# Layer 1's two lists of steps put into another order

## The chip, the cores and the metric

The kernel runs on one core of a Trainium2 chip. The metric is the time of one execution in microseconds (us) on the device. The kernel before took 2359.34 us, the median of three runs (2358.97 to 2359.86).

A core has engines that run side by side, each through its own instructions in order: PE (TensorE, matrix products and transposes), DVE (VectorE), ACT (ScalarE), POOL (GpSimd) and SP (SyncE, which here only issues DMAs). ACT and POOL issue DMAs too. An instruction that has to wait for another engine or for a transfer holds up all that stands behind it on its own engine. PSUM is the memory that PE writes its results to; it has eight banks of 128 x 512 numbers here.

## The reference, cut to what matters

The input x is 8 batches of 512 channels and 1024 tokens (32 x 32), all float32. Layer 0 is a GroupNorm, attention with 8 heads, a projection and a residual. The change leaves it alone. Layer 1 takes the output of layer 0:

```python
xf = x.reshape(B, C, N)
q, kk, v = wq @ xf, wk @ xf, wv @ xf                    # per batch, 512 x 512 weights
importance = nan_to_num(sum(xf * xf, axis=1))
_, topk_idx = top_k(importance, 256)
q_sel, k_sel, v_sel = q[topk], kk[topk], v[topk]        # 256 tokens x 512
q_sel, k_sel = layer_norm(q_sel), layer_norm(k_sel)
attn = softmax(clip(nan_to_num(q_sel @ k_sel.T * C ** -0.5), -80, 80))
out = v.at[topk].set(attn @ v_sel)                      # other tokens keep their v
return x + (wo @ out).reshape(B, C, H, W)
```

So each batch of layer 1 ranks its 1024 tokens by their squared length, runs attention among the best 256, and writes the result back into the values of all tokens.

## The kernel before

Layer 0 ends, and layer 1 begins, at about 1910 us. Layer 1 works batch by batch. One batch is cut into small steps; each is a function (lines 277 to 675) named by a word and a number, such as `row3` or `exp0`. The steps of a batch, in the order in which data passes through them:

- load (L243, SP) brings x of a batch, 2 MB in four chunks; the trace calls the chunks x, x_q, x_k. Two batches can be held; the load of the next one waits until the last reader of the old one is done.
- row 0 to 7 (L277, PE) transposes 128 tokens, four transposes into one PSUM bank; square (L282, ACT) writes squares into a tile xT and sums them; keep (L289, ACT) overwrites xT with the tokens; put (L293, a DMA issued by ACT, 256 KB) writes xT to device memory (sx). There are four xT tiles, so a square waits until the put four back has landed.
- finite (L296, DVE), spread (L304, PE, four transposes), imp (L312, ACT) and count (L317, DVE, eight steps) rank the tokens. place, pick (DVE), holder (PE) and who (DVE) turn ranks into the list of the best 256 tokens.
- xs (L402, POOL) builds sums of blocks of x; va to vf (L412, PE) compute the values of all tokens in seven products a quarter (Strassen-like), with the weights Wv and Wo already multiplied; va is eight matmuls, each other one four. ka, kb, kc, ke (L426, ACT) and kf, kg, kd (L430, DVE) take the results to V. vput (L437, a DMA issued by ACT, 256 KB) writes V to device memory (sv).
- getx and getv (L476, POOL) gather the chosen rows of x and V, two indirect DMAs each.
- selt (L500, PE) transposes the gathered x, selk (L508, ACT) copies it, qk 0 to 3 (L516, PE, 4 matmuls of 512 columns) computes queries and keys; stats (DVE), root (L534, ACT), norm (L539, DVE), normt (L555, PE) and scale (L565, ACT) are the layer norm.
- score (L577, PE), clip (L587, DVE), exp (L600, ACT), probt (L611, PE), probk (L619, ACT), att (L626, PE) and attk (L634, ACT) are the attention; attput (L641, SP) writes the result to device memory (sa); fetch 0 to 7 (L647, POOL, indirect DMAs) copies the result rows over the chosen rows of V.
- back 0 to 7 (L660, PE) transposes V; add (L670, DVE) adds the residual and issues the output DMA and the load of a later residual on SP.

Every PE step that writes PSUM takes a bank from a ring of eight (class Ring): the bank freed first is taken first, and it is freed by a named step (`keep`, `imp`, `selk`, `norm`, `scale`, `clip`, `probk`, `attk`, `add`, the last value copy, `who`). So a step of PE can also wait for a copy that belongs to quite another step.

The order of all this is written out by hand. `BATCH` (L65) is one iteration of the steady state, 180 words; `END` (L79) is the last stretch, 462 words, in which batches 4 to 7 run out. A word's number is the step's index; each "-" means one batch behind and each "+" one batch ahead of the iteration's batch. `layer1` (L700) expands them:

```python
for t in range(-1, B - 2):
    if 1 <= t:
        steps.append(("load", t + 1, 0))
    steps += [(name, t + ahead, i) for name, ahead, i in order
              if 0 <= t + ahead and (t + ahead or name not in EARLY)]
steps.append(("load", B - 1, 0))
steps += [(name, B - 1 + ahead, i) for name, ahead, i in in_order(END)]
```

The steps are then issued in this order under a manual schedule: each engine and each DMA queue executes its own steps in the order of the list, and waits only for data, tiles and banks. So what matters of a list is the order of the words that belong to one engine, and how much work of that engine lies between a step and what it waits for. In this text, (5,0) behind a step's name means batch 5, index 0.

Of the kernel before, what the change touches and what calls it, by code (L numbers as in the profile page):

```python
# [62 lines left out]


BATCH = """  # L65
back6--- row3 square1 xs1 back4--- keep2 square3 back7--- va1 inv-- put2 va0 keep3 put4 row0
keep1 add6--- ka1 add7--- ka0 put1 put3 att0-- xs0 vb1 vb0 kb0 vc0 row6 square0 kb1 add4---
square6 holder- vd0 who- add3--- kc0 keep6 row7 keep0 row5 square5 kg0 vd1 att1-- keep5 square7
getx- keep7 ve0 finite kf1 kc1 attk1-- kf0 va2 attk0-- xs2 attput-- fetch7-- kd0 fetch4--
spread0 imp0 vc1 fetch3-- ka2 spread1 va3 selt0- imp1 selk0- count1 fetch6-- count7 selt1-  # L70
selk1- fetch2-- vb2 kg1 vf1 fetch5-- vput1- count4 kf2 qk1- ke1 count0 ve1 qk0- qk2- xs3 ka3
put0 stats1- vb3 kd1 root1- back5-- norm1- stats0- kb2 put7 vput2- vput4- fetch1-- count3 vput5-
add5-- stats2- root0- qk3- norm0- vd2 vput7- vput0- stats3- root2- kc2 fetch0-- back1-- kb3
root3- vf0 normt0- vput6- ke0 norm2- vd3 back2-- back0-- normt1- vput3- put5 add1-- scale0-
scale1- vc2 vf2 norm3- normt2- count6 ke2 getv- vc3 normt3- add2-- kc3 kg2 add0-- scale2- kg3
scale3- score0- count2 score1- put6 row4+ square4+ ve3 clip- row1+ row2+ keep4+ ve2 exp0- kd3
vf3 kd2 kf3 probt- count5 place back3-- pick1 square2+ pick0 ke3 probk-
"""
END = """  # L79
square1- inv--- row7- keep2- back6---- put4- row6- put2- keep1- square7- xs3- row3- row0-  # L80
att1--- put1- keep7- put7- square3- holder-- add3---- row5- attk1--- va3- keep3- square5- row0
keep5- square0- who-- square6- put5- back7---- back4---- vput2-- add7---- finite- add6----
att0--- keep6- spread0- spread1- getx-- add4---- ka3- imp0- row7 keep0- row1 selt0-- imp1- row4
selk0-- square7 selt1-- kf3- put3- put0- selk1-- keep7 count4- count3- vput7-- square4 square1
put7 keep4 xs2- qk0-- count0- attk0--- stats0-- qk1-- count6- va2- stats1-- keep1 attput---
put6- fetch5--- count5- ka2- root1-- kf2- square0 norm1-- keep0 vput4-- qk2-- vb3- vb2- put1
fetch1--- stats2-- put0 row2 kb2- row6 count2- put4 root2-- square2 vd2- square6 row3 kb3- qk3--
fetch7--- square3 keep2 fetch2--- norm2-- fetch6--- count1- kc2- vf2- root0-- vc2- norm0-- row5
vput6-- ke2- square5 kg2- keep3 normt0-- vd3- keep5 kc3- stats3-- root3-- vput1-- vc3- count7-
# [15 lines left out]
fetch6-- attput- score0 fetch2- kb3 add6-- vd3 fetch1- fetch0- va1 score1 fetch4- clip vsel0  # L105
back3-- back5-- ka1 vselk0 fetch6- kc3 kg3 exp0 ve2 fetch5- xs0 back1-- vf2 fetch7- add3-- probt
add1-- fetch3- va0 kd2 ke2 back2-- probk ka0 inv att0 att1 attk0 ve3 attk1 back7-- vb0 xs1 kb0
vb1 add5-- add2-- attput kb1 kf1 vc0 vd0 fetch2 back4- vd1 add7-- kc0 kc1 kf0 vf0 kg0 vc1 add4-
fetch6 kd3 ve0 back6- fetch3 kg1 ve1 kd0 ke0 back3- back1- add6- fetch4 fetch0 kd1 fetch1 vf1
# [1529 lines left out]
```

## Time and profile before

| | us |
|---|---|
| median of three runs | 2359.34 |
| the profiled execution | 2355.33 |
| its span, first to last instruction | 2353.0 |
| around the span | 2.33 |
| layer 1 in the trace | about 1910 to 2353 |
| one iteration of BATCH | 56.8 |
| PE busy in the span | 2317.2 (98%) |
| DVE, ACT, POOL busy | 1875.6, 1479.1, 1432.8 |
| granted TensorE clock, mean | 0.999 |

In the rows of a timeline the first number is the start in us, the second the length in us, then the engine, the line of the kernel, the operation with output and inputs by the program's names, the shape and the number of instructions put together in the row. A bracket at the end is idle time of the engine just before, with what ended it. Matmuls are pipelined, so a row of four that is 1.03 us long is followed by the next 0.87 us after its start. In a table of stages the columns are the stretch, its length, the busy time of each engine with the number of instructions, the granted clock (1.00 is full speed), the busy share of the DMA engines and what they moved in GB/s. In the chain of waits a DMA's length is the time from its issue to its landing.

### The profile page before, as it was taken

The page shows a single profiled execution, that of the slowest core. Times are in us where ns is not written, and L with a number is a line of the kernel's source. Part 1 is how long each engine was busy: PE and PEld are TensorE (multiplying, and loading weights), DVE is VectorE, ACT ScalarE, POOL GpSimd, SP SyncE. Part 2 cuts the span into 40 slices and gives each one's busy share as a digit, 9 for nine tenths or more (in the row PEclk, how much of TensorE's full clock was granted, in tenths as well). Part 3 has the DMA queues.
Part 4 walks back from the last instruction along what each step waited for, and adds up shares of the span by engine and source line. Part 5 has one row for each costly group of instructions (what it writes and reads, how often), then busy time and mean ns, then how long its engine had stood idle before and what let it go on. Part 6 is the DMA issues. An engine that isn't in the chain of part 4 may idle for free.

```text
span 2353.0 us, 36692 instructions
## 1 busy us (share of the span) xinstructions
PE 2317.2 (98%) x13164; PEld 1053.6 (45%) x13164; DVE 1875.6 (80%) x3020; ACT 1479.1 (63%) x2024; POOL 1432.8 (61%) x890
## 2 busy tenths in 40 slices
PE   7999999999999999999999999999999999999998
PEld 3333443344344334433443344334433357777766
DVE  4889988988898888888988898888787456777774
ACT  3678766776777577757776777677666534444632
POOL 2668655866676677657765776676556724444334
PEclk9999999999999999999999999999999999999999
DMA  5112222322231222222322222222323443666655
GB/s 197 48 44 67 75 76 70 102 69 73 79 96 53 82 82 89 59 79 79 91 69 77 89 82 60 84 68 55 102 82 117 139 170 118 224 217 226 225 171 173
DMA packets 201236, 244.41 MB, mean 104 GB/s; under 512 B 41930, under 2 KB 111306, under 8 KB 201056
## 3 DMA queue, kind: packets, MB, share of 16 engines
q1 hardware_dynamic: 175392, 198.51, 26.5%
q10 hardware_dynamic: 18144, 31.48, 3.7%
q0 software_dynamic: 7520, 12.09, 1.9%
q8 instruction: 104, 1.70, 0.3%
q14 instruction: 76, 0.62, 0.1%
HBM read 181.42 MB, written 73.14 MB: 108 GB/s over the span
## 4 chain that ended last, share of the span: by engine, by line
PE 89%; DVE 4%; DMA 2%; ACT 2%; issue 2%; POOL 1%; SPq 0%; ACTq 0%; DVEq 0%; POOLq 0%
PE sc L1278 19%; PE av L1358 17%; PE g L1034 15%; PE g L899 10%; PE g L1076 7%; PE b_px L412 4%; PE b_pp L520 4%; DVE high L1292 2%; PE b_py L412 1%; PE den L1374 1%; PE b_sc L582 1%; PE first L899 1%; PE b_pa L629 1%; DVE e L1339 1%; PE last L899 1%
## 5 line engine op out<-in xcount | busy, mean ns | idle before, releaser
L1347 POOL TENSOR_TENSOR es<-es,e 128x1024 f32<-128x1024 f32 x384 | 911.1, 2373 | 167.7 <-ACT e L1342 149.8
L1339 DVE TENSOR_TENSOR e<-e,ns 128x1024 f32<-128x1024 f32 x512 | 611.3, 1205 | 7.3 <-ACT ns L1335 7.3
L1286 ACT COPY e<-sc 128x1024 f32<-128x1024 f32 x512 | 501.7, 1016 | 170.2 <-DVE high L1292 101.7
L1342 ACT ACTIVATE e<-e 128x1024 f32<-128x1024 f32 x512 | 533.3, 1063 | 91.4 <-DVE e L1339 83.9
L1292 DVE TENSOR_TENSOR high<-sc,high 128x1024 f32<-128x1024 f32 x384 | 469.4, 1222 | 121.3 <-PE sc L1278 95.9
L1278 PE MATMUL sc<-q,k 64*128 64x512 f32 x2048 | 512.3, 617 | 4.1 <-DVE high L1292 2.5
L1358 PE MATMUL av<-e,v 128*64 128x512 f32 x2048 | 489.8, 598 | 0.6 <-ACT e L1342 0.5
L1347 POOL TENSOR_TENSOR es<-e,e 128x1024 f32<-128x1024 f32 x64 | 152.5, 2382 | 435.8 <-ACT e L1342 435.8
L1278 PEld LDWEIGHTS sc<-q,k 64*128 64x128 f32 x2048 | 174.5, 186 | 269.9 <-issue 146.9
L1358 PEld LDWEIGHTS av<-e,v 128*64 128x64 f32 x2048 | 135.8, 137 | 292.5 <-issue 235.2
L1034 PE MATMUL g<-wqkv,mix_qk 128*64 128x512 f32 x960 | 231.0, 602 | 1.3 <-POOL wqkv L944 1.3
L899 PE MATMUL g<-o,wp 128*64 128x512 f32 x912 | 206.8, 596 | 0.0
L1034 PE MATMUL g<-x,mix_qk 128*64 128x512 f32 x720 | 169.8, 593 | 0.2 <-ACT v L1093 0.2
L1034 PEld LDWEIGHTS g<-wqkv,mix_qk 128*64 128x64 f32 x960 | 60.9, 136 | 155.2 <-issue 115.7
L899 PEld LDWEIGHTS g<-o,wp 128*64 128x64 f32 x912 | 63.0, 137 | 135.4 <-issue 132.9
L520 PE MATMUL b_pp<-w,selT 128*128 128x512 f32 x256 | 114.0, 593 | 0.0
L1292 DVE TENSOR_TENSOR high<-sc,e 128x1024 f32<-128x1024 f32 x64 | 77.6, 1213 | 38.0 <-ACT e L1286 37.6
L1034 PEld LDWEIGHTS g<-x,mix_qk 128*64 128x64 f32 x720 | 51.6, 137 | 103.3 <-issue 89.7
L648 POOL DMA_INDIRECT V<-sa,at x64 | 64.6, 1009 | 54.1 <-issue 15.2
L426 ACT COPY V<-b_px 128x256 f32<-128x256 f32 x112 | 39.7, 374 | 88.4 <-PE b_px L412 81.2
L1410 POOL TENSOR_TENSOR o<-o,ri 128x512 f32<-128x512 f32 x64 | 81.8, 1278 | 20.8 <-ACT o L1405 10.5
L1303 DVE STREAM_TRANSPOSE mT<-high 128x512 f32<-128x512 f32 x128 | 90.3, 705 | 1.7
(228 smaller groups left out, 2811.1 us busy)
## 6 DMA issues: line engine op xcount, KB each, us to landing
nb<-negd SPq DMA_DIRECT2D x128, 256.0 KB, 3.7
x<-in_x_dram SPq DMA_DIRECT2D x32, 512.0 KB
ri<-rid SPq DMA_DIRECT2D x128, 128.0 KB, 2.9
sx<-xT ACTq DMA_DIRECT2D x64, 256.0 KB, 2.4
mix_qk<-mixd SPq DMA_DIRECT2D x120, 128.0 KB, 2.5
xr<-in_x_dram SPq DMA_DIRECT2D x58, 256.0 KB, 3.3
x1d<-xr SPq DMA_DIRECT2D x58, 256.0 KB, 2.4
sv<-V ACTq DMA_DIRECT2D x56, 256.0 KB, 2.4
```

The costliest lines, as they stand in the source:

```text
L412: nc.tensor.matmul(out_, left, w["products"][n][:, k], start=(first and k == 0), stop=(k == 1), skip_group_check=True,)
L520: nc.tensor.matmul(pp, tiles["selT", b][:, k, ts(rb, P)], w["qk"[which]][:, k, :], start=(k == 0), stop=(k == CT - 1),)
L899: nc.tensor.matmul(out[r, :], wide_[:, r], moving, start=(k == 0), stop=(k == CT - 1),)
L1034: nc.tensor.matmul(pt[r, :], weights[:, k, r], moving[:, k, :], start=(first and k == 0), stop=(k == 1), skip_group_check=True,)
L1076: nc.tensor.matmul(pt[ts(r, HD), ts(j, P)], tokens[:, k, j * P + r * HD : j * P + r * HD + HD], weights[:, k, :], start=(first and j + k = ...
L1278: nc.tensor.matmul(sc[:, hh, :], ks[p][r, ts(j, P)], qs[p][r, ts(hf, HALF)], start=True, stop=True,)
L1286: nc.scalar.copy(raw[t, j], banks["s", t, j])
L1292: nc.vector.tensor_tensor(high[t], banks["s", t, j], raw[t, 0] if j == 1 else high[t], ALU.max)
L1339: nc.vector.tensor_tensor(raw[t, j], raw[t, j], high[t], ALU.add)
L1342: nc.scalar.activation(raw[t, j], raw[t, j], AF.Exp, scale=QK_SCALE)
L1347: nc.gpsimd.tensor_add(sums[t], raw[t, 0] if j == 1 else sums[t], raw[t, j])
L1358: nc.tensor.matmul(avs[t][HD * hh : HD * hh + HD, :], vs[p // 2][:, j, (p % 2) * P + HD * hh : (p % 2) * P + HD * hh + HD], e[:, hh, :], s ...
```

## The change

Only the two strings are changed. Each holds the same words as before, 180 and 462, each as often, so every engine executes the same instructions on the same data; their order on each engine is another. The lists were rearranged in small moves, and their maker kept to at most three of ScalarE's transfers (put, vput) on the way at a time. Nothing in the code enforces that number: it is a property of the order. BATCH is shown whole; of END, the parts around its beginning, batch 5's exp and probt, batch 7's gather and the last words.

```diff
@@ -63,52 +63,53 @@
 BATCH = """
-back6--- row3 square1 xs1 back4--- keep2 square3 back7--- va1 inv-- put2 va0 keep3 put4 row0
-keep1 add6--- ka1 add7--- ka0 put1 put3 att0-- xs0 vb1 vb0 kb0 vc0 row6 square0 kb1 add4---
-square6 holder- vd0 who- add3--- kc0 keep6 row7 keep0 row5 square5 kg0 vd1 att1-- keep5 square7
-getx- keep7 ve0 finite kf1 kc1 attk1-- kf0 va2 attk0-- xs2 attput-- fetch7-- kd0 fetch4--
-spread0 imp0 vc1 fetch3-- ka2 spread1 va3 selt0- imp1 selk0- count1 fetch6-- count7 selt1-
-selk1- fetch2-- vb2 kg1 vf1 fetch5-- vput1- count4 kf2 qk1- ke1 count0 ve1 qk0- qk2- xs3 ka3
-put0 stats1- vb3 kd1 root1- back5-- norm1- stats0- kb2 put7 vput2- vput4- fetch1-- count3 vput5-
-add5-- stats2- root0- qk3- norm0- vd2 vput7- vput0- stats3- root2- kc2 fetch0-- back1-- kb3
-root3- vf0 normt0- vput6- ke0 norm2- vd3 back2-- back0-- normt1- vput3- put5 add1-- scale0-
-scale1- vc2 vf2 norm3- normt2- count6 ke2 getv- vc3 normt3- add2-- kc3 kg2 add0-- scale2- kg3
-scale3- score0- count2 score1- put6 row4+ square4+ ve3 clip- row1+ row2+ keep4+ ve2 exp0- kd3
-vf3 kd2 kf3 probt- count5 place back3-- pick1 square2+ pick0 ke3 probk-
+keep2 back7--- put4 square1 row3 xs1 va1 back4--- square3 back6--- va0 keep3 keep1 add4--- xs0
+add7--- put1 put2 ka1 add3--- add6--- ka0 put3 att0-- row0 vb0 kb0 vb1 vc0 square0 kb1 row6
+square6 holder- vput1- who- getx- vd0 row7 keep6 kc0 row5 keep0 square5 vput6- att1-- kg0 inv--
+vd1 square7 finite ve0 attk0-- kf0 kc1 xs2 attk1-- kf1 attput-- fetch6-- va2 fetch4-- spread1
+keep5 spread0 keep7 va3 vc1 ka2 fetch2-- vput7- imp1 imp0 fetch5-- vb2 vf1 kd0 selt0- count1
+selt1- selk0- selk1- kg1 ve1 count7 fetch7-- qk1- ke1 qk2- ka3 count0 kf2 count4 vput0- fetch1--
+put7 fetch0-- stats1- xs3 back5-- kd1 root1- qk0- count3 vput3- stats2- fetch3-- norm1- vput2-
+qk3- vb3 stats0- vput4- root0- kb2 add5-- norm0- root2- put0 kb3 vd2 vd3 stats3- vput5- root3-
+normt1- kc2 normt0- back1-- scale0- vf2 scale1- vf0 back0-- back2-- norm2- put5 norm3- vc2 kc3
+add1-- normt2- normt3- add0-- scale2- vc3 count6 ke2 add2-- scale3- kg3 kg2 score1- score0-
+count2 getv- put6 row4+ clip- ve3 ke0 kd3 kf3 vf3 ve2 square4+ kd2 count5 row2+ keep4+ row1+
+exp0- place probt- square2+ back3-- pick0 ke3 probk- pick1
 """
 END = """
-square1- inv--- row7- keep2- back6---- put4- row6- put2- keep1- square7- xs3- row3- row0-
-att1--- put1- keep7- put7- square3- holder-- add3---- row5- attk1--- va3- keep3- square5- row0
-keep5- square0- who-- square6- put5- back7---- back4---- vput2-- add7---- finite- add6----
-att0--- keep6- spread0- spread1- getx-- add4---- ka3- imp0- row7 keep0- row1 selt0-- imp1- row4
-selk0-- square7 selt1-- kf3- put3- put0- selk1-- keep7 count4- count3- vput7-- square4 square1
-put7 keep4 xs2- qk0-- count0- attk0--- stats0-- qk1-- count6- va2- stats1-- keep1 attput---
...
-va0- ve2- scale0-- fetch0--- vput5-- fetch4--- finite norm3-- normt1-- fetch3--- spread1 kd2-
-ka0- put5 imp1 normt3-- normt2-- xs0- scale3-- spread0 kg3- place- pick1- vf3- scale1-- va1-
-keep6 pick0- imp0 back7--- holder- scale2-- score1-- score0-- count5 vb0- back6--- who- ve3-
-count3 clip-- kb0- vd0- back0--- ka1- getx- back3--- ke3- vput3-- add6--- kf0- vput0-- xs1- vb1-
-add7--- back2--- add3--- kc0- put6 selt0- vf0- vc0- exp0-- add2--- kd3- count6 inv-- selt1-
-selk0- vput3- count4 selk1- qk1- probt-- probk-- put2 count7 qk2- kg0- getv-- att0-- attk0--
-count1 count2 count0 kb1- place att1-- put3 pick1 ve0- vd1- ke0- pick0 attk1-- stats1- qk0- kd0-
-holder vc1- stats0- attput-- who back1--- back5--- kc1- kg1- vf1- root1- ve1- ke1- getx add1---
-qk3- vput4- stats2- kd1- va2 kf1- add5--- vput0- norm1- selt0 root0- vput6- fetch2-- norm0-
-selk0 back4--- add4--- selt1 ka2 selk1 vput5- normt0- stats3- fetch4-- fetch3-- root2- norm2-
-qk2 vput1- stats2 normt1- qk0 root3- kf2 vput2- fetch1-- fetch0-- norm3- qk1 va3 root2 xs3
-scale1- xs2 scale0- normt3- norm2 stats1 stats0 scale3- root1 normt2- scale2- ka3 qk3 vb2 kb2
-score0- add0--- vput7- root0 score1- stats3 norm0 root3 vd2 norm3 getv- back4-- clip- exp0-
-normt2 back0-- scale2 norm1 vb3 vsel1 inv- probt- add4-- kf3 normt0 add0-- normt3 probk- normt1
-fetch7-- scale1 scale3 att0- attk0- kc2 back6-- vselk1 att1- vc2 kg2 vc3 fetch5-- scale0 attk1-
...
-vf3 ke1 fetch5 back5- back2- back7- back0- back4 add3- back6 add1- add2- add5- back2 add0- back0
-ke3 fetch7 add7- add4 add6 back5 add2 back1 back7 add0 back3 add5 add7 add3 add1
+back6---- xs3- row7- row0- square1- row3- put4- square7- keep2- att1--- keep1- row6- holder--
+put2- add3---- inv--- keep7- row5- row0 who-- put1- put7- back7---- square3- attk1--- keep3-
+va3- square6- square5- square0- keep5- vput2-- att0--- finite- row7 put5- keep0- add6----
+add7---- back4---- put3- add4---- keep6- ka3- kf3- getx-- spread0- imp0- spread1- imp1- row1
+square7 selt0-- selk0-- row4 selt1-- count3- attk0--- put6- selk1-- count4- keep7 qk0-- vput6--
+vput4-- count0- qk1-- put7 stats0-- count6- stats1-- va2- square1 count5- root1-- vput7-- xs2-
...
+vd3- norm2-- kg2- stats3-- keep2 square6 row5 square5 count7- root3-- normt0-- ke2- va0- vc3-
+vput5-- fetch4--- ve2- keep5 finite scale0-- normt1-- norm3-- kd2- kc3- kg3- vput1-- spread1
+scale1-- normt2-- spread0 vput3-- normt3-- place- pick1- imp1 keep6 fetch1--- scale3-- xs0- vf3-
+imp0 va1- ka0- pick0- holder- fetch3--- scale2-- count5 ka1- score0-- vb0- vput0-- who- kb0-
+back7--- score1-- getx- put5 kf0- back6--- ve3- back3--- count3 clip-- ke3- back0--- vd0-
+add3--- xs1- vb1- kc0- back2--- exp0-- selt0- vf0- add6--- kb1- kd3- add2--- put6 probt-- vc0-
+count4 kg0- selt1- selk0- count7 selk1- put2 qk1- getv-- count6 add7--- inv-- count0 count1
+count2 probk-- qk2- att0-- place attk0-- att1-- stats1- pick0 pick1 ke0- attk1-- attput-- qk0-
+stats0- ve0- vput3- kd0- vd1- holder vc1- back1--- put3 who root1- kc1- kg1- kf1- root0- vf1-
+fetch0-- back5--- ve1- add1--- qk3- getx ke1- norm1- norm0- va2 add5--- vput5- stats2- selt0
+selt1 vput4- va3 kd1- selk0 back4--- fetch4-- selk1 stats3- normt1- qk2 xs2 add4--- root2- ka2
+normt0- norm2- stats2 root3- root2 qk1 vput7- norm3- scale1- qk0 kf2 fetch1-- normt2- stats1
+vput6- root1 norm2 scale2- stats0 normt3- scale3- ka3 vput2- vb2 norm1 qk3 vput0- xs3 fetch3--
+stats3 root0 scale0- kb2 vb3 add0--- norm0 score0- root3 norm3 score1- vd2 fetch2-- back4--
+vput1- kc2 fetch5-- clip- exp0- normt2 getv- scale2 vsel1 kf3 fetch7-- add4-- probt- back0--
+probk- normt3 normt0 vselk1 fetch6-- scale3 att0- normt1 att1- back6-- inv- attk0- scale1 vc2
...
+kf1 back1- vf3 kd1 fetch1 back2- ke1 fetch5 back5- add3- back7- back0- back4 add1- back6 back2
+add5- add7- add0- ke3 add2- back0 fetch7 add4 add6 add2 add0 back7 back3 add7 back1 add3 back5
+add5 add1
 """
```

More of the change, by code (lines that the diff above doesn't have):

```diff
@@ L81 @@
-att1--- put1- keep7- put7- square3- holder-- add3---- row5- attk1--- va3- keep3- square5- row0
-keep5- square0- who-- square6- put5- back7---- back4---- vput2-- add7---- finite- add6----
-att0--- keep6- spread0- spread1- getx-- add4---- ka3- imp0- row7 keep0- row1 selt0-- imp1- row4
-selk0-- square7 selt1-- kf3- put3- put0- selk1-- keep7 count4- count3- vput7-- square4 square1
-put7 keep4 xs2- qk0-- count0- attk0--- stats0-- qk1-- count6- va2- stats1-- keep1 attput---
-put6- fetch5--- count5- ka2- root1-- kf2- square0 norm1-- keep0 vput4-- qk2-- vb3- vb2- put1
@@ L87 @@
-fetch1--- stats2-- put0 row2 kb2- row6 count2- put4 root2-- square2 vd2- square6 row3 kb3- qk3--
-fetch7--- square3 keep2 fetch2--- norm2-- fetch6--- count1- kc2- vf2- root0-- vc2- norm0-- row5
-vput6-- ke2- square5 kg2- keep3 normt0-- vd3- keep5 kc3- stats3-- root3-- vput1-- vc3- count7-
-va0- ve2- scale0-- fetch0--- vput5-- fetch4--- finite norm3-- normt1-- fetch3--- spread1 kd2-
-ka0- put5 imp1 normt3-- normt2-- xs0- scale3-- spread0 kg3- place- pick1- vf3- scale1-- va1-
-keep6 pick0- imp0 back7--- holder- scale2-- score1-- score0-- count5 vb0- back6--- who- ve3-
@@ L105 @@
[L105 to L109, printed above, removed]
-vf3 ke1 fetch5 back5- back2- back7- back0- back4 add3- back6 add1- add2- add5- back2 add0- back0
@@ new lines @@
+vput4-- count0- qk1-- put7 stats0-- count6- stats1-- va2- square1 count5- root1-- vput7-- xs2-
+put0- square4 qk2-- ka2- vb3- kf2- norm1-- keep1 keep4 put1 row3 vb2- row6 square0 row2
+attput--- fetch2--- kb2- keep0 stats2-- kb3- root0-- fetch0--- vd2- root2-- qk3-- square3
+fetch7--- kc2- put0 count2- fetch5--- vf2- fetch6--- keep3 put4 norm0-- count1- square2 vc2-
+vd3- norm2-- kg2- stats3-- keep2 square6 row5 square5 count7- root3-- normt0-- ke2- va0- vc3-
+vput5-- fetch4--- ve2- keep5 finite scale0-- normt1-- norm3-- kd2- kc3- kg3- vput1-- spread1
@@ new lines @@
+vput1- kc2 fetch5-- clip- exp0- normt2 getv- scale2 vsel1 kf3 fetch7-- add4-- probt- back0--
+probk- normt3 normt0 vselk1 fetch6-- scale3 att0- normt1 att1- back6-- inv- attk0- scale1 vc2
+attk1- vc3 kb3 scale0 score0 va1 add6-- score1 attput- fetch0- fetch6- clip fetch1- kg2 vsel0
+vd3 kc3 fetch2- fetch4- kg3 vf2 ve2 vselk0 fetch5- kd2 back1-- xs0 ke2 back5-- exp0 add1--
+back3-- probt probk add3-- va0 fetch7- att0 add0-- fetch3- back2-- inv ka1 att1 attk0 ka0 attk1
+ve3 vb0 add5-- vc0 back7-- xs1 vb1 attput kb0 kf0 kb1 fetch2 vd0 back4- add2-- vd1 kc0 vf0 vc1
@@ L112 @@
+kd3 fetch6 kc1 kg0 ve0 add7-- fetch3 back6- add4- ke0 kg1 ve1 kd0 fetch4 back3- vf1 add6- fetch0
+kf1 back1- vf3 kd1 fetch1 back2- ke1 fetch5 back5- add3- back7- back0- back4 add1- back6 back2
+add5- add7- add0- ke3 add2- back0 fetch7 add4 add6 add2 add0 back7 back3 add7 back1 add3 back5
+add5 add1
 """
```

## The prediction

> **What bounds the kernel now.** I read the shares of busy time first, then the work by stage of Layer 1 (1909.9 to 2353 us, the only part that the change touches), then PE's timeline, ScalarE's timeline and the chain of waits.
>
> ```profile
> PE 2317.2 (98%) x13164; PEld 1053.6 (45%) x13164; DVE 1875.6 (80%) x3020; ACT 1479.1 (63%) x2024; POOL 1432.8 (61%) x890
> ```
> PE is the bound: 98%. The change adds and removes no PE instruction, so all it can win is PE's idle time in Layer 1. The stages (us from:to, length, then busy time of PE, PEld, DVE, ACT, POOL, granted clock, share of the DMA engines, GB/s):
>
> ```profile
> 1909.90:1928.40 18.50, 16.77 (x109) 14.51 (x110) 4.92 (x21) 12.13 (x32) 6.30 (x12) 1.00 0.77 271
> 2077.40:2134.20 56.80, 56.63 (x286) 42.47 (x285) 39.59 (x125) 26.69 (x67) 26.41 (x45) 1.00 0.61 203
> 2188.80:2200.70 11.90, 10.44 (x74) 7.53 (x73) 6.12 (x26) 8.46 (x22) 5.45 (x10) 1.00 0.93 312
> 2264.00:2274.20 10.20, 10.05 (x51) 7.34 (x50) 7.57 (x25) 1.83 (x5) 7.60 (x9) 1.00 0.75 255
> 2274.20:2341.80 67.60, 67.60 (x301) 48.15 (x300) 33.78 (x88) 21.88 (x55) 33.84 (x52) 1.00 0.42 135
> 2341.80:2353.00 11.20, 4.11 (x34) 3.39 (x32) 6.61 (x12) 0.00 (x0) 0.75 (x1) 0.87 0.80 294
> ```
> Idle: 1.73 us in the opening, 0.17 in one iteration of BATCH, 1.46 where END begins, 0.15 near 2272, none for 67.6 us, and the tail. PE's timeline names the waits in brackets:
>
> ```profile
> 1922.60 1.13 PE L412 MATMUL b_py<-w,xs 128*128 128x256 f32 x4 [0.68 <-DVE V L430]
> 1926.51 0.62 PE L308 MATMUL b_pi<-ident,col 128*128 128x128 f32 x4 [1.06 <-DVE col L302]
> ...
> 2187.74 0.33 PE L615 MATMUL b_ppt<-ident,s 128*128 128x128 f32 x1
> 2188.23 0.55 PE L615 MATMUL b_ppt<-ident,s 128*128 128x128 f32 x3 [0.16 <-ACT s L603]
> 2188.61 0.60 PE L664 MATMUL b_po<-ident,V 128*128 128x128 f32 x4
> ...
> 2196.63 0.44 PE L280 MATMUL b_pt<-ident,x_q 128*128 128x128 f32 x2 [0.91 <-ACT att L636]
> 2198.32 0.66 PE L664 MATMUL b_po<-ident,V 128*128 128x128 f32 x4 [0.55 <-ACT xT L290]
> ```
> probt takes 0.87 us from its first start to the next step's start, where four transposes elsewhere take 0.43 to 0.44 (2272.73 to 2273.16): 0.44 us lost in each of five iterations. Adding up: 1.74 + 5 × 0.44 + 1.46 + 0.3 at 2272 = 5.7 us, 0.24% of the time. That is the ceiling of what an order can win, short of the last adds and their DMAs. Behind the waits, ScalarE and the chain:
>
> ```profile
> 1924.86 0.60 ACT L284 ACTIVATE xT<-b_pt 128x512 f32<-128x512 f32 x1 [0.52 <-DMA sx<-xT]
> 2185.79 1.28 ACT L603 ACT_TABLE_LOAD   x1
> 2187.59 0.49 ACT L603 ACTIVATE s<-s,nm 128x256 f32<-128x256 f32 x1
> 2195.31 0.60 ACT L284 ACTIVATE xT<-b_pt 128x512 f32<-128x512 f32 x1 [2.57 <-DMA sx<-xT]
> ```
> ```profile
> 2188.82 6.41 DMA sx<-xT
> ```
> A square needs the xT buffer of the put four before it, so a late landing holds ScalarE and everything queued behind it. (Later puts, in calm stretches, land in about 2.4 us by the DMA issues' median.)
>
> **The change part by part.** Removed and added: nothing. Each step is moved on its engine's queue, with all that it issues: puts and value puts on ScalarE's queue, attput, residual and output transfers on SP's, gathers, fetches and sums on GpSimd's. On ScalarE and SP an issue costs the queue 0.3 to 0.8 us wherever it stands (the put at 1913.54 held it 0.36, the x load at 2187.49 0.79), so moving them adds nothing; what counts is when they land.
>
> *Opening, −0.7.* The two waits cost 0.68 + 1.06. spread(1,0) waits for finite, which waits for square7, which waits for put3 (issued 1917.14, landed 1924.84). The new list issues put4, put1 and put2 a copy or two earlier, but put3 still follows ka0. square7 now stands ahead of keep5, so it no longer sits behind one 0.58 copy: −0.6, if put3 lands no later. ve(1,0) waits for kg0, behind kc0, and kc0 now follows keep6: +0.6 on a wait that shrinks as the other squares start earlier. I take −0.7: the 0.6 and a little of the earlier landings. Bounds: −1.74 (both go) to +0.6 (the kc0 copy shows whole).
>
> *The five steady iterations, +0.1 each, +0.5.* row4+ still follows score, square4, keep4, the 1.28 load and the exp still follow it, and probt keeps its PE cover: the 0.44 stays. What the new list shortens: only ve1 (four matmuls, 0.87) stands between selt1 and qk1, where two such steps stood; selt1's second copy ended at 2098.49 and qk1 began at 2099.38, so 0.89 of slack becomes 0.02. vd3 follows vd2 at once, 0.87 after vb3, with kb3 behind root0 and root2 on ScalarE. score's bank, freed by scale2, has three transpose steps (1.30) between. att1 is 0.87 earlier and takes the bank of keep6, behind square6, where 0.68 was spare. Each is about at zero slack; I take 0.1 an iteration, bounds 0 to 0.5 (0 to +2.5 in all). I see no gain: the steps run back to back already. GpSimd's xs3 now follows seven fetches instead of six (+1.30, the spacing of gathers at 2264.66 and 2265.97), attput is about 1.1 us earlier and add5's transposes 4.3 us earlier, each covered by slack of 3 us and more; cost 0, and if the slack were wrong, up to the one 1.30 on xs3, inside the upper bound. getv's wait for the value puts stays off PE's path: 0.
>
> *END's head, −1.0.* row(7,0) waits for attk(4,1), which stands behind square(6,3), which waited 2.57 for the put issued at 2188.82. The last x load of the loop on SP goes out when the last vf3 has read x. vf3 now stands ahead of row1, row2 and ve2 (0.43 + 0.43 + 0.87 = 1.73 us of PE work), so the load leaves about 1.7 us sooner (it went at 2187.49) and clears the DMA engines sooner; the put itself moves ahead of keep2 (0.58). I expect the landing 1.0 to 1.7 earlier; the waits 0.91 + 0.55 shrink by 1.0. Bounds: −1.46 (all) to +0.15 (same landing, with va3 now the one that waits for attk's bank).
>
> *Inside END.* probt(5,0) moves 4.7 us earlier on PE, to about 2245.5, while its exp ended at 2245.69, after the last ScalarE copy ahead (2243.01), a 1.28 table load and two exponentials: a new wait of +0.4 (0 to +0.5). getx(7): who(7) comes about 1.7 us earlier, but one fetch (1.30) now stands ahead of it, waiting for attput's landing; net 0.5 earlier, so the 0.31 wait of selt(7,0) goes: −0.3 (−0.31 to +0.9, where that fetch waits). Other bank waits with no slack left (row1 and row7, normt3, qk3, back0 behind clip, normt2 behind norm3): +0.3 (0 to +1.0, one 0.5 copy at two of them). The tail keeps 19.5 us of PE work after the last att, eight fetches and twelve adds in a row: 0 (0 to +0.5). The table loads and the groups of roots keep their count.
>
> *Sum.* −0.7 + 0.5 − 1.0 + 0.4 − 0.3 + 0.3 + 0 = −0.8 on a profiled execution of 2355.33 us (span 2353.0 and 2.33 around it): 2354.5. That execution is 4.0 us (0.17%) under the median of the runs, 2359.34, so I put the same difference on the median: 2358.5. All best ends: −1.74 − 1.46 − 0.31 = −3.5, 2355.8. All worst: 0.6 + 2.5 + 0.15 + 0.5 + 0.9 + 1.0 + 0.5 = +6.2, 2365.5.
>
> [...]
>
> [...]
>
> **The rivals.**
>
> *The shorter distances show whole (slower).* Place: qk1 behind selt1's copy, and vd3 behind kb3, in each iteration. Each loses 0.87 of cover. For it: the slack of 0.02 worked out above, and ScalarE is often late by a copy. Against it: that copies and table loads could shift with PE. Price: 0.87 in five iterations is +4.35 in place of +0.5, 2362.4; with both places 2366.7. It is slower by over 0.2% (4.7 us, about what a measurement tells from no change) from 1.2 us an iteration.
>
> *The landing at END's head does not move (same).* Contention and not the load's start sets it. For it: the puts of the opening took as long, 7.70 us. Then −1.0 becomes +0.15: 2359.7.
>
> *All waits on transfers go (faster).* For it: both stages have them on the chain. Against it: put3 still follows ka0. −3.5, 2355.8; over 0.2% only if the five probt waits (2.2) went too, 2353.6, for which I see no step moved.
>
> **How the numbers follow.** Chances: forecast 0.55; shorter distances 0.25, of which 0.15 over the bound; landing unmoved 0.15; faster 0.05, of which 0.03 over the bound. So faster 0.03, slower 0.15, same 0.82. The predicted time is the likeliest case's 2358.5. The range takes the all-best sum, 2355.8, and reaches into the first rival to 2364.0, leaving out some 0.13 there and 0.03 below.
>
> **What would show it.** Right: PE's count unchanged; at END's head the wait of the first row below 0.5 and ScalarE's square below 2 us of waiting; probt with 0.4 us lost in each iteration and a new wait at 2245. Wrong: brackets of 0.3 us or more at qk1, vd3, score or att1 in every iteration, or puts that land later than before because they go out in closer groups.

## The result, and the profile after

The changed kernel takes 2369.09 us (median of 6 runs) against 2358.45 us for the kernel before, in runs side by side. The medians are 10.6 us apart. The ratio on record is 1.0058, with a 95% interval of 1.0048 to 1.0068, so the change makes the kernel slower by 11 to 16 us. Its profiled execution took 2368.34 us, with a span of 2366.5. Layer 1, from its first `row` to the end of the span, grew from 443.1 us (1909.87 to 2353.0) to 458.1 us (1908.36 to 2366.5).

The shares of busy time of the kernel after:

```profile
PE 2319.9 (98%) x13164; PEld 1055.6 (45%) x13164; DVE 1873.9 (79%) x3020; ACT 1478.0 (62%) x2024; POOL 1433.2 (61%) x890
```

PE has as many instructions as before, and no other engine has come near to being the bound. The time went into waits. The same stages, cut where they begin in the new trace (stretch, length, busy time of PE, PEld, DVE, ACT, POOL, granted clock, DMA share, GB/s):

```profile
1908.40:1926.90 18.50, 16.13 (x105) 13.83 (x106) 4.42 (x19) 11.78 (x32) 5.66 (x10) 1.00 0.77 271
2078.96:2137.72 58.76, 56.57 (x285) 42.58 (x285) 38.99 (x123) 26.56 (x67) 26.40 (x45) 1.00 0.58 198
2355.00:2366.50 11.50, 3.82 (x31) 3.35 (x31) 6.53 (x11) 0.00 (x0) 1.13 (x2) 0.91 0.84 312
```

In the opening PE is idle for 2.37 us (18.50 - 16.13) where it was 1.73, and in the last stage for 7.68 (11.50 - 3.82) where it was 7.09. One iteration of BATCH is 58.76 us long where it was 56.76, and PE is idle for 2.19 us of it (58.76 - 56.57) where it was 0.17. PE's timeline shows one place for that, the same in all five iterations (here the one that begins at 2020.2), and two of the longer waits outside of them:

```profile
1915.57 1.99 PE L413 MATMUL b_px<-tvo,xs 128*128 128x256 f32 x8 [1.36 <-ACT V L427]
...
2075.65 1.03 PE L413 MATMUL b_py<-w,xs 128*128 128x256 f32 x4
2078.87 1.13 PE L413 MATMUL b_px<-tvo,x_k 128*128 128x256 f32 x4 [2.19 <-DVE V L431]
...
2081.57 0.60 PE L616 MATMUL b_ppt<-ident,s 128*128 128x128 f32 x4
2082.01 1.04 PE L665 MATMUL b_po<-ident,V 128*128 128x128 f32 x8
...
2356.60 2.18 PE L665 MATMUL b_po<-ident,V 128*128 128x128 f32 x18 [1.67 <-DMA V<-sa,at]
```

The row at 2078.87 is vf3. It follows ve3 (2075.65), which is four matmuls, 0.87 us in all, so it could have begun at 2076.52; it began 2.35 us later. Behind it probt no longer waits (2081.57 to 2082.01 is 0.44), since exp had run in the meantime: 2.35 + 0.1 (vf3's row is 1.13 us long, the rows on either side of it 1.03) - 0.44 = 2.0 us an iteration, 10.0 us in five. What vf3 waited for is an add of VectorE to V; the rows of VectorE there:

```profile
2075.42 0.69 DVE L592 TENSOR_SCALAR sfin<-b_sc 128x512 f32<-128x512 f32 x1 [0.99 <-PE b_sc L583]
2076.03 0.68 DVE L594 TENSOR_SCALAR s<-b_sc 128x512 f32<-128x512 f32 x1
2076.74 0.69 DVE L595 SCALAR_TENSOR_TENSOR s<-s,sfin 128x512 f32<-128x512 f32 x1
2077.47 0.69 DVE L596 TENSOR_REDUCE nm<-s 128x2 f32<-128x512 f32 x1
2078.07 0.41 DVE L431 TENSOR_TENSOR V<-b_py,V 128x256 f32<-128x256 f32 x1
2078.40 0.41 DVE L431 TENSOR_TENSOR V<-b_px,V 128x256 f32<-128x256 f32 x1
```

The first four are clip, which cannot start before score ends; the fifth is kd3 and the sixth kf3, which ends 0.06 us before vf3 begins. In the old list the order of the two was the other one, and VectorE waited for PE, in a place where PE waits for nothing of VectorE's. vf3 and the same kf3 in the kernel before:

```profile
2130.11 1.03 PE L412 MATMUL b_px<-tvo,x 128*128 128x256 f32 x4
...
2131.17 0.42 DVE L430 TENSOR_TENSOR V<-b_px,V 128x256 f32<-128x256 f32 x1 [0.44 <-PE b_px L412]
```

kf3 reads the second half of the bank px, vf3 adds to the first half, so no number passes between them. In both kernels the later of the two waits for the earlier one all the same, kf3 for vf3 with a bracket of 0.44 us in the kernel before and vf3 for kf3 with one of 2.19 us in the changed one: these programs keep the order for the bank, not for the half. What would happen without that order no run here shows. A list of the pairs on one bank that changed sides, made from the diff, would have shown the swap.

Three more us come from the clock. After two of the five waits at vf3 PE ran at half its clock for 3.4 us. Behind the wait that ended at 2196.39, and behind the equal one that ended at 2137.63:

```profile
2197.40:2200.70 3.30, 3.30 (x13) 2.73 (x13) 1.25 (x4) 0.40 (x1) 0.00 (x0) 0.51 0.72 204
2137.70:2141.00 3.30, 3.30 (x23) 3.04 (x24) 1.34 (x4) 1.52 (x8) 3.03 (x8) 1.00 0.33 81
```

13 matmuls in 3.30 us at a clock of 0.51 against 23 at 1.00. In the two places with a stretch of half clock (the other is at 1961.8) 4.4 us pass from vf3's start to probt's, in the three others 2.7: 1.7 us lost in each. So of 15.0 us of longer layer 1, the waits at vf3 are 10.0, the clock behind them 3.4, and the opening (brackets of 1.36, 0.77 and 0.24 against 1.74) 0.6; the rest, 1.0, lies in END.

### The profile page after: what moved, and what is told of

It reads as the page before. It is cut to its first block, busy times and chain, and to the rows that moved or that the text cites. A ratio compares the mean times of both kernels' runs of the same rounds, so it can differ in the third digit from the quotient of the medians.

```text
span 2366.5 us, 36691 instructions
## 1 busy us (share of the span) xinstructions
PE 2319.9 (98%) x13164; PEld 1055.6 (45%) x13164; DVE 1873.9 (79%) x3020; ACT 1478.0 (62%) x2024; POOL 1433.2 (61%) x890
## 4 chain that ended last, share of the span: by engine, by line
PE 89%; DVE 5%; DMA 2%; ACT 2%; issue 1%; POOL 1%; ACTq 0%; SPq 0%; POOLq 0%; DVEq 0%
PE sc L1279 19%; PE av L1359 17%; PE g L1035 15%; PE g L900 10%; PE g L1077 7%; PE b_pp L521 5%; PE b_px L413 5%; DVE high L1293 2%; PE b_py L413 2%; PE den L1375 1%; PE b_sc L583 1%; DVE e L1340 1%; PE first L900 1%; PE b_pa L630 1%; PE last L900 1%
## 5 line engine op out<-in xcount | busy, mean ns | idle before, releaser
L1305 DVE TENSOR_REDUCE quarter<-mT 128x16 f32<-128x512 f32 x128 | 87.8, 686 | 4.4
```

## The experiments

The runs were made on three chips, on which the kernel before takes 2356 to 2362 us. Each has the time of the kernel before on its own chip beside it, and between chips only the ratios compare.

**The new lists with two words swapped.** This undoes the one suspected thing and leaves the rest of the change.

```diff
-count2 getv- put6 row4+ clip- ve3 ke0 kd3 kf3 vf3 ve2 square4+ kd2 count5 row2+ keep4+ row1+
+count2 getv- put6 row4+ clip- ve3 ke0 kd3 vf3 kf3 ve2 square4+ kd2 count5 row2+ keep4+ row1+
```

> The new lists with two neighbouring words of BATCH swapped, kd3 kf3 vf3 -> kd3 vf3 kf3. Theory A (vf3 waits for kf3, which stands behind clip on VectorE): the bracket of 2.2 us ahead of vf3 goes from all five iterations, the period falls from 58.76 to about 56.8 us, and with the two stretches of halved clock behind it the time falls by 10 to 13 us, to 2356 - 2359. Theory B (the wait is for kd3, whose rows have the same line and the same tile V): kd3 still stands ahead of vf3, so nothing changes, 2368 - 2370. Theory C (the iteration is longer because its covers were shortened at qk1, vd3 and score): at most 2 us of the 10.6 come back, about 2367.

Measured: 2357.84 us, against 2362.25 for the kernel before on the same chip; ratio 0.9986 (0.9977 to 0.9995). The period is back, and so is probt's wait. A stage of one iteration, and PE's rows of it:

```profile
2072.75:2129.50 56.75, 56.59 (x284) 42.68 (x284) 39.40 (x124) 26.38 (x66) 26.47 (x44) 1.00 0.61 206
```
```profile
2069.69 1.03 PE L413 MATMUL b_px<-tvo,x_k 128*128 128x256 f32 x4
...
2072.79 0.55 PE L616 MATMUL b_ppt<-ident,s 128*128 128x128 f32 x3 [0.17 <-ACT s L604]
```

vf3 (2069.69) has no bracket although kd3 still stands ahead of it, so theory B falls. The whole loss is gone and a little more, so theory C falls too. One swap of neighbours was the difference between a slower kernel and one that is not slower.

**The old lists with the pair in the new order.** Is it enough by itself? Three words are moved: the pair also stands directly behind ve3 on PE, as in the new list, and no longer behind row1, row2 and ve2.

```diff
-scale3- score0- count2 score1- put6 row4+ square4+ ve3 clip- row1+ row2+ keep4+ ve2 exp0- kd3
-vf3 kd2 kf3 probt- count5 place back3-- pick1 square2+ pick0 ke3 probk-
+scale3- score0- count2 score1- put6 row4+ square4+ ve3 clip- kd3 kf3 vf3 row1+ row2+ keep4+ ve2
+exp0- kd2 probt- count5 place back3-- pick1 square2+ pick0 ke3 probk-
```

> The old lists with three words of BATCH moved: kd3 kf3 vf3 stand directly behind clip, ahead of row1, row2, keep4 and ve2, so that kf3 stands ahead of vf3. Theory A: this alone makes most of the loss; vf3 waits some 2.3 us in each iteration, the 0.44 us wait of probt is swallowed by it, +2.0 us an iteration, +10 us in all, and up to 3 us more where the clock drops behind a wait: 2368 - 2372. Theory C: the covers at qk1, vd3 and score are the old ones, so within 1 us of the old kernel.

Measured: 2371.39 us against 2362.25, ratio 1.0036 (1.0022 to 1.0049). The five waits are there, 2.35 us each, with all other covers as they were:

```profile
2079.10 1.16 PE L412 MATMUL b_px<-tvo,x_k 128*128 128x256 f32 x4 [2.19 <-DVE V L430]
2080.07 1.89 PE L280 MATMUL b_pt<-ident,x 128*128 128x128 f32 x8
2081.75 1.89 PE L412 MATMUL b_py<-w,xs 128*128 128x256 f32 x4
```

Behind this wait PE was slower: four matmuls take 1.89 us (2081.75) that take 1.03 elsewhere, as in the stretches of half clock above (1.91 at 2197.50 in the changed kernel). Three of the five waits of this execution were followed by that, with 1.4 to 1.7 us each; its mean granted clock is 0.997, where the kernel before has 0.999. So the pair, in this place, is enough to bring the five waits, and the swap before shows that it is needed. In time this run lost 5 to 12 us by its interval, where the whole change lost 11 to 16; no run tells whether anything else takes part in that difference.

**kf3 ahead of clip.** The pair stays in the new order; only what kf3 waits behind is taken away.

```diff
-count2 getv- put6 row4+ clip- ve3 ke0 kd3 kf3 vf3 ve2 square4+ kd2 count5 row2+ keep4+ row1+
+count2 getv- put6 row4+ kf3 clip- ve3 ke0 kd3 vf3 ve2 square4+ kd2 count5 row2+ keep4+ row1+
```

> The new lists with kf3 moved ahead of clip in BATCH; kf3 still stands ahead of vf3. Theory A with the four passes of clip (4 x 0.69 us) as the cause of the lateness: kf3 runs in the idle time that VectorE has before score ends (1.0 us there), vf3 finds it done, and the time is that of the swapped kernel within 1 us, 2356 - 2359. Theory A without clip (vf3 after kf3 costs by itself, or by ve3): the bracket stays over 1 us and the time over 2363.

Measured: 2357.76 us, ratio 0.9984 (0.9975 to 0.9993), the same as the swap. VectorE does the add in the time in which it would have waited for score:

```profile
2067.58 0.42 DVE L431 TENSOR_TENSOR V<-b_px,V 128x256 f32<-128x256 f32 x1
2068.64 0.69 DVE L592 TENSOR_SCALAR sfin<-b_sc 128x512 f32<-128x512 f32 x1 [0.64 <-PE b_sc L583]
```

So a kf ahead of its vf costs nothing; a kf ahead of its vf, behind the four passes of clip, and with no work of PE between ve3 and vf3, costs 2.35 us.

**vf3 back behind 1.73 us of PE work.** kf3 stays ahead of vf3 and behind clip.

```diff
-count2 getv- put6 row4+ clip- ve3 ke0 kd3 kf3 vf3 ve2 square4+ kd2 count5 row2+ keep4+ row1+
-exp0- place probt- square2+ back3-- pick0 ke3 probk- pick1
+count2 getv- put6 row4+ clip- ve3 ke0 kd3 kf3 ve2 square4+ kd2 count5 row2+ keep4+ row1+ vf3
+exp0- place probt- square2+ back3-- pick0 ke3 probk- pick1
```

> The new lists with vf3 moved behind row1+ in BATCH, so that kf3 still stands ahead of vf3, but ve2, row2 and row1 (0.87 + 0.43 + 0.43 = 1.73 us of PE work) stand between ve3 and vf3. Theory A (what is lost is what PE has no work for): the bracket falls from 2.35 to 0.6 us, and as exp runs on meanwhile, probt's wait of 0.44 goes; +0.2 us an iteration on the kernel with vf3 ahead of kf3, ratio to before 0.999 to 1.0. No wait reaches 2 us, so no stretch of halved clock follows in the iterations. If vf3 behind kf3 costs something of its own, the bracket stays near 2 us and the ratio near 1.005.

Measured: 2361.31 us against 2356.02, ratio 1.0024 (1.0015 to 1.0033). The wait itself came out as worked out, the time did not:

```profile
2015.48 1.13 PE L413 MATMUL b_px<-tvo,x 128*128 128x256 f32 x4 [0.45 <-DVE V L431]
2016.45 0.60 PE L616 MATMUL b_ppt<-ident,s 128*128 128x128 f32 x4
...
2031.19 1.98 PE L630 MATMUL b_pa<-vs,sT 128*128 128x512 f32 x4 [1.10 <-ACT xT L291]
```

vf3 begins 0.61 us late (2.35 - 1.73 = 0.62) and probt's wait is gone. But att1 waits for a bank that `keep6` frees, 1.26 us late here and 1.79 us at 2147.13, and END's head waits 2.62 us at 2199.91. The chain of waits that leads to att1, and ScalarE's rows in it:

```profile
2017.02 4.64 DMA x<-x1d
2021.66 0.02 issue
2021.68 8.49 DMA y<-x1d
...
2030.19 0.33 ACTq L439 DMA_DIRECT2D sv<-V  x1
2030.56 0.59 ACT L291 COPY xT<-b_pt 128x512 f32<-128x512 f32 x1 [1.88 <-DMA y<-x1d]
```

keep6 (2030.56) stands on ScalarE behind the issue of vput1, and that issue stood until 2030.17, when a residual load landed that SP had issued at 2021.68. No number passes between the two. The rows show the release, 8.49 us after the load's issue, and not its cause. In the trace of the kernel before, an issue that stands the same way can be followed further: in layer 1 the transfers of SP and of ScalarE name the same eight semaphores there (100 to 106 and 108), and put3's issue at 1917.14 waits for 101, which it is going to use itself and which the residual load issued at 1912.72 used; that load landed at 1917.12. That vput1 stood for the same cause is inferred from this. In the swapped kernel the same residual load left at 2021.49 and landed after 6.07 us. The wait at 2147.13 has the same chain; the one at 2199.91 stands behind a square that waited 3.73 us for a put. With vf3 later, the load of x that waits for it left at 2017.02 instead of 2014.37, while probt came only 0.9 us later; three of the four puts behind it landed 7.4 to 8.4 us after their issue, where in the swapped kernel three of the four took 5.0 to 5.6 (the first put is the other way round, 4.8 against 8.1). So the earlier vf3 has a use: the new order has so little cover at att1 that it needs the early load. That the slower landings follow from the later load is argued from the times of the loads and landings; no run changes the load alone.

**The two lists apart.** The old BATCH with the new END, and the new BATCH (with vf3 ahead of kf3) with the old END; the lists are exchanged whole.

> The old BATCH with the new END. Summed from the brackets of PE in the two profiles, END's waits went from 3.2 to 5.3 us (the fetches at the end 1.1 -> 3.0, a vf1 that waits 0.74 for a kf1 ahead of it, and 0.3 to 0.5 elsewhere, against 1.8 saved at its head). If that is all, +1 to +3 us on the old kernel, 2359.5 - 2361.5, and no iteration has a wait at vf3. If END's loss depends on what the new BATCH leaves it (the late x load, the clock), it is within 1 us of the old kernel.

> The new BATCH with vf3 ahead of kf3, and the old END. Against the first kernel of these runs (the same BATCH with the new END) this tells what the new END does. By the brackets of PE the new END waits more (5.9 us in that kernel's trace, of them 2.9 for the last fetches, against 3.2 in the old kernel), so the old END would be about 2 us faster, ratio to before 0.9978. By the times of the old BATCH with the new END (ratio 0.9989) the new END is the better one by 2.6 us, so the old END would bring the time back up, ratio 0.9997.

Measured: 2359.03 against 2362.25, ratio 0.9989 (0.9980 to 0.9998), for the new END under the old BATCH; 2353.21 against 2356.11, ratio 0.9990 (0.9981 to 0.9999), for the old END under the new BATCH. Both expectations from the brackets miss: the new END is not slower. Beside the swapped kernel's 0.9986 (0.9977 to 0.9995) the two ENDs cannot be told apart. The brackets overstate END, because PE is not what ends the kernel: from PE's last transpose to the end of the span there are 6.3 us with the old END (the kernel before) and 4.4 with the new one (the swapped kernel), in which the last adds and output DMAs run. A late PE at the end is partly made good there.

The second run also tells the size of one step of the prediction by itself, END's head under an x load that leaves 1.74 us sooner, counted from probt:

```profile
2193.47 0.44 PE L280 MATMUL b_pt<-ident,x_q 128*128 128x128 f32 x2
...
2195.16 0.66 PE L664 MATMUL b_po<-ident,V 128*128 128x128 f32 x4 [0.55 <-ACT xT L290]
```

Of 0.91 + 0.55 the first is gone. The put landed 6.53 us after probt's first transpose, 7.49 before: 0.96 earlier. That it is the load which did this is argued, as the new BATCH moves other transfers too.

**The changed kernel again**, beside the others on one chip.

> The changed kernel as it is, beside the others on one chip. Theory A: five waits of 2.35 us at vf3, period 58.76 us, ratio to before 1.004 to 1.006, and 1.3 to 1.7 us more behind each wait after which the clock drops: two in its first trace, a number that differs from execution to execution.

Measured: 2368.61 us against 2356.11, ratio 1.0063 (1.0047 to 1.0078). Five waits of 2.35 us again, the period 58.76 again, and this time one stretch of half clock (behind the wait that ended at 2134.95) instead of two; the mean granted clock is 0.998, in the first trace 0.997. Its span is 2363.3 where the first trace's is 2366.5.

**Three other waits of the new lists moved.** Beside the swap: in BATCH put1 and put2 go behind ka0, in END kf1- behind vf1-, and for the last batch kf1 behind kb1 and kd1 behind kd0.

```diff
-add7--- put1 put2 ka1 add3--- add6--- ka0 put3 att0-- row0 vb0 kb0 vb1 vc0 square0 kb1 row6
+add7--- ka1 add3--- add6--- ka0 put1 put2 put3 att0-- row0 vb0 kb0 vb1 vc0 square0 kb1 row6
...
-stats0- ve0- vput3- kd0- vd1- holder vc1- back1--- put3 who root1- kc1- kg1- kf1- root0- vf1-
+stats0- ve0- vput3- kd0- vd1- holder vc1- back1--- put3 who root1- kc1- kg1- root0- vf1- kf1-
...
-ve3 vb0 add5-- vc0 back7-- xs1 vb1 attput kb0 kf0 kb1 fetch2 vd0 back4- add2-- vd1 kc0 vf0 vc1
-kd3 fetch6 kc1 kg0 ve0 add7-- fetch3 back6- add4- ke0 kg1 ve1 kd0 fetch4 back3- vf1 add6- fetch0
-kf1 back1- vf3 kd1 fetch1 back2- ke1 fetch5 back5- add3- back7- back0- back4 add1- back6 back2
+ve3 vb0 add5-- vc0 back7-- xs1 vb1 attput kb0 kf0 kb1 kf1 fetch2 vd0 back4- add2-- vd1 kc0 vf0
+vc1 kd3 fetch6 kc1 kg0 ve0 add7-- fetch3 back6- add4- ke0 kg1 ve1 kd0 kd1 fetch4 back3- vf1
+add6- fetch0 back1- vf3 fetch1 back2- ke1 fetch5 back5- add3- back7- back0- back4 add1- back6
```

> The new lists with vf3 ahead of kf3, and the three other waits that its trace shows moved: in BATCH put1 and put2 behind ka0 (the wait of 1.52 us at 1915); in END kf1- behind vf1- (0.76 us at 2264), and for the last batch kf1 behind kb1 and kd1 behind kd0, so that kd1 no longer stands behind a kf1 that waits for vf1 (the gathers at the end lost 1.4 us there). Theory A (each is a wait that PE sees): 1.1 + 0.7 + 1.4 = 3.2 us less than with the first swap alone, ratio to before 0.9972. Rival: the waits move to the next late step, and less than 1 us is won, ratio 0.9982 to 0.9986.

Measured: 2354.23 us against 2356.11, ratio 0.9996 (0.9987 to 1.0005): no gain over the swap. The waits moved. At the opening they go from one place to the next. The swapped kernel has 1.36 at 1915 and 0.25 at 1924; this one has:

```profile
1915.00 1.99 PE L413 MATMUL b_px<-tvo,xs 128*128 128x256 f32 x8 [0.22 <-ACT V L427]
1923.11 1.13 PE L413 MATMUL b_py<-w,xs 128*128 128x256 f32 x4 [1.73 <-DVE V L431]
1926.40 0.84 PE L309 MATMUL b_pi<-ident,col 128*128 128x128 f32 x6 [0.43 <-DVE col L303]
```

1.36 became 0.22, and 1.73 came up at ve(1,0): ScalarE stood 3.62 us before a square until the put issued there landed at 1921. At the end the gathers' loss of 1.3 us is gone (their last issue is at 2341.45 in place of 2342.41), and so is the wait of vf1-; but the adds behind the last gathers run back to back at 0.60 us each, and the time from the last issue to the end of the span went from 11.05 to 11.66 us.

**The same with keep4 behind exp.**

```diff
-count2 getv- put6 row4+ clip- ve3 ke0 kd3 vf3 kf3 ve2 square4+ kd2 count5 row2+ keep4+ row1+
-exp0- place probt- square2+ back3-- pick0 ke3 probk- pick1
+count2 getv- put6 row4+ clip- ve3 ke0 kd3 vf3 kf3 ve2 square4+ kd2 count5 row2+ row1+ exp0-
+keep4+ place probt- square2+ back3-- pick0 ke3 probk- pick1
```

> The same with keep4+ behind exp0- in BATCH, so that ScalarE's table load and exp no longer wait for that copy of 0.59 us. Theory: the exp then waits for clip alone, ends about 0.3 us sooner, and probt's wait of 0.44 falls to 0.1 in five iterations: 1.7 us less, ratio to before 0.9965. Rival: the bank that keep4 frees comes 2 us later and a transpose step waits for it, so nothing is won or up to 1 us an iteration is lost, ratio 0.9972 to 0.9993.

Measured: 2354.53 us against 2356.11, ratio 0.9993 (0.9984 to 1.0002). ScalarE does what was expected:

```profile
2070.20 1.28 ACT L604 ACT_TABLE_LOAD   x1
2071.83 0.51 ACT L604 ACTIVATE s<-s,nm 128x256 f32<-128x256 f32 x1 [0.35 <-DVE nm L596]
```

exp now waits for clip (0.35) and no longer for the table load. probt has lost all but 0.1 us of its wait, and no bank is missed. In its trace layer 1 is 440.8 us long, 3.4 less than without this move, but only 5 x 0.3 = 1.4 to 1.5 of that is this wait; the times of the two, on one chip, do not differ by more than their intervals.

**What these point to together:** that BATCH with the old END.

> The new BATCH with vf3 ahead of kf3, put1 and put2 behind ka0, and keep4+ behind exp0-, with the old END. By the brackets: 1.0 us less at the opening and 5 x 0.3 us less at probt than with the new BATCH and old END alone (ratio 0.9990), so ratio 0.998. Rival: these waits are no longer what sets the time there, ratio 0.999.

Measured: 2353.65 us against 2356.02, ratio 0.9989 (0.9980 to 0.9998). Its trace is the shortest of all (span 2348.2, layer 1 439.9 us). It is faster than the kernel before and than the changed one, but no faster than the single swap can be told to be.

**The kernel before once more.**

> The kernel before once more, unchanged: what two runs of one kernel differ by, and a second trace of it. Ratio 1.000 within 0.001; five waits of 0.44 at probt, and at the opening, the head of END and the last gathers waits within 1 us of the first trace's.

Measured: 2355.62 against 2356.02, ratio 0.9998 (0.9989 to 1.0007). Layer 1 is 444.2 us long in this trace, 443.1 in the first; the opening alone differs, with waits of 2.6 and 1.0 us where the first trace has 1.2 and 0.8, more than the expected 1 us. In both, the issue of put3, with all of ScalarE behind it, stood until a residual load landed that SP had issued, at 1917.12 in the first trace and at 1917.88 in this one, which is 7.25 and 9.39 us after the start of layer 1.

## Why the prediction was wrong

The forecast was 2358.5 us with 0.82 on no change; the kernel takes 2369.09 us, and the range ended at 2364.0.

The step that failed is the term of the five steady iterations: "+0.1 each, +0.5", bounded by 0.5 an iteration. It measured +2.0 an iteration, +10.0, with 3.4 us of half clock behind it in the first trace and one such stretch instead of two in the second. The list of shortened covers named qk1, vd3, score and att1 and did not name vf3. That vf3 had moved was seen, and priced at END's head, but only for what it lets go sooner, the load of x ("vf3 now stands ahead of row1, row2 and ve2"). What it now waits for was not asked: kf3, which had stood behind it, stands ahead of it on the list, and kf3's queue on VectorE holds clip. What is queued ahead of the thing a moved step waits for was asked at qk1, vd3, score and att1, and left out where the queue is longest. "I see no gain" held; that nothing beside the four could lose was never shown.

The first rival had the right kind of mechanism, a cover in each iteration that comes out whole, and its point of decision, 1.2 us an iteration, was passed by the 2.0. Its place was wrong: in no iteration has qk1, vd3, score or att1 a bracket in the trace after. Its price with one place, 2362.4, was too low: it took 0.87 of lost cover, where vf3 has nothing at all between ve3 and itself and the whole 2.35 shows.

The other steps, as far as the runs tell:

| step | forecast, us | measured, us |
|---|---|---|
| opening | -0.7 | +0.6 in the changed kernel's first trace, -0.1 in its second and in the swapped one (1.36 + 0.25 against 1.74); the kernel before itself differs by 1.5 between its two traces |
| iterations beside vf3 | +0.5 | 0 (56.75 against 56.76 each) |
| END's head | -1.0 | -1.0 under the old END; -0.3 under the new one, counted over the spacing of back-to-back matmuls |
| probt(5,0) | +0.4 | +0.3 |
| getx(7) | -0.3 | -0.3 in the changed kernel, -0.1 in the swapped one |
| other waits of END | +0.3 | +0.7 at vf1- behind kf1-, and 0.2 to 0.4 elsewhere |
| tail | 0 | PE waits 2.0 more for gathers, of which most is made good behind PE's end |

At the opening the mechanism failed: put1 and put2 ahead of the value copies were counted as an earlier issue that costs the same wherever it stands, but ScalarE ran no copy for 1.04 us there, 0.8 of it in the two issues, and vb waited for ka1 behind them. Nor was it ka0 that held put3: in the trace before, its issue waited until 1917.12 for a residual load on the same semaphore (101). At END's head the landing came 0.96 us earlier under the old END, just under the 1.0 to 1.7 that were forecast. The other half of that step was wrong: the put did not gain the 0.58 of keep2. It is issued 1.09 us (old END) or 1.14 us (new END) after probt's first transpose, 1.08 before, and in the trace before it leaves at 2188.82 although keep2's copy, ahead of it on the list, begins at 2189.96. Under the new END attk's bank is then waited for by another step, va3, which is what the upper bound had. In END the two waits that were missed have the same cause as vf3: kf1- ahead of vf1- (0.57 in brackets), and kf1 of the last batch, which stood ahead of kd1 and waited for vf1, so that the gather behind kd1 lost 1.3 us.

With the one swap undone, the rest of the change is worth what the sum said in kind: no change that reaches 0.2% (ratio 0.9986, where the forecast of -0.8 us is 0.9997, just above its interval). In the traces its layer 1 is 1 to 2 us longer than before (445.2 against 443.1 and 444.2), in the times it is 3 us shorter. The time outside of the span explains 0.5 us of the 3: over all runs on record its median is 1.9 us, against 2.4 before. The granted clock explains none: its mean over these runs is 0.998 in both. The spans themselves differ by 3.5 us in the median (2355.9 against 2359.4), and a trace shows one execution of each; where the 3 us lie stays open.

## What to carry to other kernels

When an order is changed, list for every moved step its neighbours that changed sides, and for each such pair ask which engine now waits, what is queued ahead of the partner, and how much work of the waiting engine covers it; a step that moves forward gains at its readers and loses at its writers, and both belong in the sum. Steps of two engines on one PSUM bank were such a pair here although they touch different halves of it (with kf3 behind clip and ahead of vf3 PE waited 2.35 us an iteration, with kf3 behind vf3 not at all): let the engine with time to spare be the one that waits. A transfer's issue was such a place too: ScalarE stood 1.4 us at put3 in the kernel before (1915.76 to 1917.14), and 1.5 us at vput1 with vf3 behind row1+ (2028.67 to 2030.19), until a transfer of SP's had landed. A wait that was moved along where something else was late next gave back little of its bracket: at the opening 1.36 us became 0.22, and 1.73 came up behind it. It was the same in front of the tail, which PE does not end: 1.3 us went at the last gathers, and the time behind them grew by 0.6.

## What the hardware showed that was not expected

PE's clock fell behind waits of about 2 us, and not each time. In the traces of the kernel before and of the changed kernel (from 1840 us on) PE waited seven times for 2.0 to 2.4 us: 2.05 at 1847 in both, and five times 2.35 in the changed one. Behind three of these seven (1847 in the trace before, the waits that ended at 1961.41 and 2196.39 in the one after) it ran at half clock for 3.41 us, which cost 1.7 us at each of the two in the one after. Behind the seven waits of 1.0 to 1.9 us in these traces it never did. Equal waits in one execution differ: of the five of 2.35 us, two were followed by it. The wait of 2.05 us at 1847, at the end of layer 0, which the change leaves alone, was followed by it in the trace before and not in the one after, so it may also be a part of what executions of one kernel differ by.

The clock's own records in the two traces tell which waits these are. Every stretch of half clock before the last few us of the kernel is 3.413 us long: the one at 1848.37 in the trace before, those at 60.45, 1961.68 and 2197.20 in the one after. With the one that each kernel ends in (2350.13 and 2364.45) they begin whole multiples of 3.4133 us apart: 147 in the trace before; 557, 69 and 49 in the one after. So each trace can be laid out in windows of 3.4133 us. Two equal waits of the changed kernel in these windows (stretch, length, busy time of PE, PEld, DVE, ACT, POOL, granted clock, DMA share, GB/s):

```profile
2135.76:2139.17 3.41, 1.54 (x7) 1.39 (x8) 1.78 (x4) 2.53 (x6) 3.25 (x7) 1.00 0.01 4
2139.17:2142.58 3.41, 3.41 (x30) 3.26 (x29) 2.82 (x12) 2.49 (x8) 2.21 (x6) 1.00 0.76 233
...
2193.78:2197.20 3.42, 1.23 (x6) 0.75 (x6) 2.48 (x5) 3.24 (x8) 2.62 (x5) 1.00 0.72 278
2197.20:2200.61 3.41, 3.41 (x13) 2.84 (x12) 1.16 (x4) 0.31 (x1) 0.00 (x0) 0.50 0.67 187
```

The wait that ended at 2137.63 began at 2135.28, ahead of its window, which holds 1.87 us of idle PE; no half clock follows. The one that ended at 2196.39 lies whole in its window, with 2.19 us of idle PE; the next window runs at half clock. It is so in all seven: the idle time of each of the three waits that were followed by half clock lies in one window, and each of the four others has 0.4 to 1.1 us of it in a second window. In these two traces, whether a wait of this length costs 1.7 us more thus goes with where it falls in the windows, and these lie differently: counted in steps of 3.4133 us from the start of the span, they begin 1.75 us behind a step in the trace before and 2.42 in the one after. This was read from the traces afterwards; no run moved a wait on purpose to try it.
